# A graph kernel on one core: other due times for VectorE's order, a second buffer for the spread keys, one round fewer for the fourth block's list

## The chip, the cores and the metric

The kernel runs on one core of a Trainium2 chip. The metric is the device time of one execution in microseconds (us). The profile is one execution recorded on the chip; its times are counted from the first instruction of that execution. Engines are named as in the profile: PE is TensorE, PEld its weight loads, DVE is VectorE, ACT is ScalarE, POOL is GpSimd, SP is SyncE, which issues most plain DMAs.

## What is computed

Sixteen graphs of 1024 nodes with 64 channels go through four layers. Each layer adds to `x` a function of `relu(layernorm(x))` and of the graph's adjacency matrix. Cut to what matters:

```python
h = relu(layernorm(x)); x = x + tanh(concat(h, adj @ h) @ W1 + b1) @ W2 + b2      # layer 0
h = relu(layernorm(x)); A = adj + eye; x = x + (A @ h) / A.sum(2)                 # layer 1
h = relu(layernorm(x))                                                            # layer 2
# neighbours (adj > 0, with the node itself), thinned: of a node with m > 10 neighbours
# every ((m + 1) // 2)-th is removed, in both directions
# agg[n, c] = 0.25 q25 + 0.5 q50 + 0.25 q75 of h[neighbours of n, c]   (interpolated)
x = x + mask * (relu((h + agg) @ W1 + b1) @ W2 + b2)
h = relu(layernorm(x)); x = x + (adj @ h) / deg @ Wn + h @ Ws + b                 # layer 3
```

Layer 2 is the costly one. It needs the quantiles of each channel over a ragged set of neighbours.

## The kernel before

The nodes of a graph are put in the order of their number of neighbours and cut into 8 blocks of 128. Blocks share five groups (`GROUPS`), which hold 1, 1, 2, 2 and 2 blocks; `PLACES` says how many neighbours a block's nodes can have, 21 for the first down to 11 for the last. Per graph, six generator functions do the work:

- `adjacency` reads the matrix in 8 pieces, transposes it on TensorE into `adjt` (L947, copied by ScalarE in L948), counts neighbours (L954), works out the thinning (`gone`, L993 and L998), forms a key for each pair of nodes (L1018, L1022, L1025) and writes the keys to DRAM. Then it ranks the nodes: `key` and `neg` (L1032, L1034), two tiles `spread` (L1038) that TensorE turns into a matrix (L1040), eight passes `sink` on ScalarE that count (L1045), then `pos`, `low`, `both` (L1048 to L1062), a matmul (L1065) and `node` (L1071).
- `neighbour_lists` gathers each block's keys (`k`, POOL, L1086), takes the 8 largest with MAX8 (L1101) and then, in rounds of L1110 or L1112, L1115 and L1117, 8 more at a time. The list becomes `index`.
- `layers` does layers 0 and 1. Both hold a product with the adjacency matrix, `messages`: 32 matmuls L875 and a copy L876. The second one is issued after the `memset` L1197; behind it come L1202 and L1204 on TensorE, `den` on VectorE (L1217), and on ScalarE eight passes L1210 that sum degrees, each pair followed by a DMA that writes `adjt` to DRAM (`adjt_d`). A layer normalisation is `preln`: L846 to L848 on VectorE, the square L849 on ScalarE, L851 on VectorE, the root L852 on ScalarE, L854 and L855 on VectorE, L856 on ScalarE.
- `gathers` issues 124 gathers of neighbour rows (`raw`, POOL, L1274), one for each place of each block.
- `sorts` sorts `raw` by a network of minima and maxima on VectorE (L1307) and forms `agg` (L1324, L1326).
- `tail` brings `agg` back to node order (`res`, POOL, L1346), does the rest of layer 2 (`paired`: L883 on TensorE and L885 on ScalarE; L1355, L1356, then `per_node`: L899) and adds it to `x` on VectorE (`mid`, L1360); then layer 3, whose last product is read in L1395.

The engines run through their queues in the order in which instructions were issued, so the order of issue is the plan. It is made when the program is built. Each function is a generator that yields the time at which it wants to go on, worked out from a planned clock: `clk.dve`, `clk.pe`, `clk.act` and `clk.pool` are moved on by written costs, and `after(dve, pe, act, lat)` returns the moment when a chain over these engines should be done, plus `lat`. A loop at the end takes, in a fixed order of the six streams, the first one whose time has come; if none is due, the planned clock of VectorE jumps to the soonest. So the written costs decide what VectorE does between the issue of work for another engine and the instruction that reads its result. They are not waits: at run time an instruction waits for its data alone.

`gate` keeps POOL in step. VectorE writes a mark (L915) and POOL copies it (L917), so that POOL can't pass this place before VectorE has reached it. A gate is issued ahead of every fourth place of a group whose last mark lies over 4 us of planned time back.

Buffers come from pools. In the pool `lists` a tile has two buffers unless it says otherwise; `maskf`, `edge`, `spread`, `sink` and `low` share the tag `ab`, which has one. `adjt`, `nb` and `gone` have one each, and so has each group's `raw`.

Of the kernel before, what the change touches and what calls it, by code (L numbers as in the profile page):

```python
# [7 lines left out]
F32 = mybir.dt.float32  # L8
F16 = mybir.dt.float16
BF = mybir.dt.bfloat16  # L10
I32 = mybir.dt.int32
U16 = mybir.dt.uint16
U8 = mybir.dt.uint8
AF = mybir.ActivationFunctionType
ALU = mybir.AluOpType
AX = mybir.AxisListType

P = 128
C = 64
NB = 8  # L20
N = 1024
# [12 lines left out]
I16 = mybir.dt.int16  # L34
# [21 lines left out]
PLACES = [21, 19, 17, 16, 15, 13, 12, 11]  # L56
PACKS, NPACK = [(0, 0, 21, 2, 64), (1, 0, 23, 1, 32), (1, 32, 24, 4, 24), (2, 0, 28, 10, 12)], 3
KB = 4

# [670 lines left out]
def direct_path(ctx: ExitStack, tc: tile.TileContext, t: dict, out: bass.AP, flag):  # L730
# [3 lines left out]
    nc = tc.nc  # L734
    x_in, adj, nodemask = t["x"], t["adj"], t["nodemask"]
    B = x_in.shape[0]
# [64 lines left out]
    nc.gpsimd.dma_start(mask8, nodemask.rearrange("b (i p) -> (b i) p", p=P))  # L801
    maskf = lists.tile([B * NB, P], F32, tag="ab", name="maskf", bufs=1)
    nc.vector.tensor_copy(maskf, mask8)
# [10 lines left out]
    clk = Clock()  # L814
# [26 lines left out]
    def preln(u, x, ha):  # L841

        s = nodes.tile([P, 4, NB], F32, name="stat")
        xc = mid(u, [P, NB, C])
        sq = mid(u, [P, NB, C])
        nc.vector.tensor_reduce(s[:, 0], x, AX.X, ALU.add)  # L846
        ts(s[:, 1], s[:, 0], 1.0 / C, None, op0=ALU.mult)
        tt(xc, x, s[:, 1, :, None].to_broadcast([P, NB, C]), ALU.subtract)  # L848
        act(sq, xc, AF.Square)  # L849
        yield after(1.5, act=0.65)  # L850
        nc.vector.tensor_reduce(s[:, 2], sq, AX.X, ALU.add)  # L851
        act(s[:, 3], s[:, 2], AF.Sqrt, bias=eps, scale=1.0 / C)  # L852
        yield after(0.7, act=1.0)
        nc.vector.reciprocal(s[:, 2], s[:, 3])  # L854
        tt(xc, xc, s[:, 2, :, None].to_broadcast([P, NB, C]), ALU.mult)  # L855
        act(ha[:, :, :C], xc, AF.Relu)  # L856
        yield after(0.9, act=0.65)
# [20 lines left out]
    def paired(hs, dst):  # L878

        p = bank()  # L880
        for q in range(4):
            for e, h in enumerate(hs):
                nc.tensor.matmul(p[:, q * P:(q + 1) * P], h[:, 2 * q:2 * q + 2, :].rearrange("p u c -> p (u c)"), identf,  # L883
                                 start=e == 0, stop=e == len(hs) - 1)
        nc.scalar.copy(dst, p)  # L885
        clk.pe = max(clk.pe, clk.dve) + 1.5
        clk.act = max(clk.act, clk.pe) + 0.7
# [45 lines left out]
    def adjacency(b):  # L933
# [26 lines left out]
        sf = nodes.tile([P, 4, NB], F32, name="sf")  # L960
        yield clk.act + 0.3
        tt(mn[:, 2], mn[:, 0], mn[:, 1], ALU.add)
# [20 lines left out]
        for i in range(NB):  # L983
            following = flipped(i + 1) if i + 1 < NB else None

            p = bank2()
            for j in range(NB):
                o, e = j * P, (j // 4 + 1) * 512
                nc.tensor.matmul(p[:, o:e], nbt[:, j, :], stair[:, :e - o], start=j % 4 == 0, stop=j % 4 == 3)  # L989

            for q in range(2):
                s = slice(q * 512, (q + 1) * 512)
                act(gone[:, i, s], p[:, s], AF.Abs, bias=sf[:, 2 + q, i:i + 1], scale=2.0)  # L993
            nbt = following
            ready = after(0, pe=3.7, act=2.4)
            if waiting:
                yield waiting[1]
                ts(gone[:, waiting[0], :], gone[:, waiting[0], :], sf[:, 1, waiting[0]:waiting[0] + 1], -1.0,  # L998
                   op0=ALU.is_equal, op1=ALU.mult)
                clk.dve += 0.5  # L1000
            waiting = (i, ready)
# [27 lines left out]
        act(mv, ms, AF.Copy, bias=512.0, scale=0.5)  # L1029
        yield clk.act + 0.3  # L1030
        key = nodes.tile([P, NB], F32, name="key")
# [4 lines left out]
        for q in range(2):  # L1036
            spread = lists.tile([P, 4, P], F32, tag="ab", name="spread", bufs=1)
            tt(spread, identf[:, None, :].to_broadcast([P, 4, P]),  # L1038
               key[:, 4 * q:4 * q + 4, None].to_broadcast([P, 4, P]), ALU.mult)
            nc.tensor.matmul(p[:, q * 512:(q + 1) * 512], onesf, spread.rearrange("p j m -> p (j m)"),  # L1040
                             start=True, stop=True)
        over = nodes.tile([P, NB], F32, name="over")
        for i in range(NB):
            sink = lists.tile([P, N], F16, tag="ab", name="sink", bufs=1)
            act(sink, p, AF.Sign, bias=neg[:, i:i + 1], accum_out=over[:, i:i + 1])  # L1045
        yield after(1.6, pe=1.3, act=10.5)
        pos = nodes.tile([P, NB], I32, name="pos", bufs=5)
# [6 lines left out]
        nc.vector.tensor_copy(ph, pi)  # L1054
        low = lists.tile([P, NB, P], F16, tag="ab", name="low", bufs=1)
        tt(low, pidx[:, None, :].to_broadcast([P, NB, P]), ph[:, 0, :, None].to_broadcast([P, NB, P]), ALU.is_equal)
# [11 lines left out]
        nc.scalar.copy(m, p[:, NB:2 * NB])  # L1068
        yield after(2.3, pe=1.2, act=0.2) - 0.2
        node = nodes.tile([P, NB], I32, name="node", bufs=3)  # L1070
# [6 lines left out]
    def neighbour_lists(b):  # L1077
# [3 lines left out]
        ks = []  # L1081
# [9 lines left out]
        for i in range(KB):  # L1091
            load_keys(i)
        total = sum(n * -(-cap // 8) * 8 for _, n, cap, *_ in GROUPS)
        found = lists.tile([P, total], F32, name="found", bufs=1)
        m = g["m"]
        o = 0
        for b0, n, cap, *_ in GROUPS:
            for i in range(b0, b0 + n):
                src, at = ks[i]
                yield at  # L1100
                nc.vector.max(out=found[:, o:o + 8], in_=src)  # L1101
                clk.dve += 1.15
                yield clk.dve
                less, before = src.bitcast(I16), None
                for r in range(1, -(-cap // 8)):


                    least = found[:, o + 7:o + 8]
                    if r == 1:
                        ts(less, src, least, None, op0=ALU.subtract)  # L1110
                    else:
                        ts(less, less, before, least, op0=ALU.add, op1=ALU.subtract)  # L1112
                    before = least
                    most = nodes.tile([P, 8], U16, name="most")
                    nc.vector.max(out=most, in_=less.bitcast(U16))  # L1115
                    o += 8
                    ts(found[:, o:o + 8], most.bitcast(I16), 0.0, least, op0=ALU.min, op1=ALU.add)  # L1117
                    clk.dve += 1.8
                    yield clk.dve
                o += 8  # L1120
                load_keys(i + KB)
        index = lists.tile([P, total], I32, name="index")
# [51 lines left out]
    def layers(b):  # L1174
# [17 lines left out]
        nc.scalar.copy(x, p)  # L1192
        yield after(0, pe=1.3, act=2.1) + 2.8
        ha = nodes.tile([P, NB, C + 1], F32, name="ha")
# [18 lines left out]
        done.add(("adjt", b))  # L1213
        yield after(0, pe=10.5, act=1.1) + 2.5
        clk.act += 10
# [21 lines left out]
    def gathers(b):  # L1237
        g = state[b]
        yield max(g["rows_at"], clk.pool)
        for k, (b0, n, cap, *_) in enumerate(GROUPS):  # L1240
            while not (b == 0 or ("sort", b - 1, k) in done):
                yield None
            raw = raws.tile([P, cap, n * C], F32, name=f"raw{k}")
            o = sum(c * -(-r // 8) * 8 for _, c, r, *_ in GROUPS[:k])
            clk.pool = max(clk.pool, clk.dve)
# [6 lines left out]
            if k == 0:  # L1252
                packed = nodes.tile([P, NPACK * C], F32, name="packed", bufs=1)
                for l, size in enumerate(sizes):
                    nc.gpsimd.indirect_dma_start(packed[:size, l * C:(l + 1) * C], None, h_ds[b % 3],
                                                 bass.IndirectOffsetOnAxis(ap=g["pack"][:size, l:l + 1], axis=0))
                    clk.pool += 1.27
                rows_d = dram.tile([NPACK, P, C], F32, name="rows_d")
            for s in range(cap):
# [9 lines left out]
                for i in range(n):  # L1269
                    if s >= PLACES[b0 + i]:  # L1270
                        continue
                    clk.pool += 1.27
                    at = o + i * -(-cap // 8) * 8 + s
                    nc.gpsimd.indirect_dma_start(raw[:, s, i * C:(i + 1) * C], None, h_ds[b % 3],  # L1274
                                                 bass.IndirectOffsetOnAxis(ap=g["index"][:, at:at + 1], axis=0))
# [64 lines left out]
    def tail(b):  # L1340
# [16 lines left out]
        y = per_node(bank(), h1, w22, 8, b22)  # L1357
        yield after(0, pe=2.2, act=1.5) + 3.2
        o = mid(1, [P, NB, C])
# [17 lines left out]
        nc.scalar.copy(x, per_node(bank(), ht, w3s, 4, b3, x))  # L1377
        yield after(0, pe=3, act=0.6, lat=0.5)

# [12 lines left out]
        zn = per_node(bank(), mt, w3n, 4)  # L1392
        yield after(0, pe=2.6)
        o = mid(1, [P, NB, C])
# [16 lines left out]
    programs = [_program(*group[2:]) for group in GROUPS]  # L1411
    edge = lists.tile([1, 2, C], F32, tag="ab", name="edge", bufs=1)
    nc.vector.memset(edge[:, 0], 0.0)
# [165 lines left out]
```

## Time and profile before

| | us |
|---|---|
| median of 7 runs | 3699.97 |
| lowest, highest | 3697.49, 3700.79 |
| the profiled execution | 3697.76 |
| its span, first to last instruction | 3695.8 |
| VectorE busy | 3067.9 |
| POOL busy | 2600.5 |
| TensorE busy | 1977.2 |
| ScalarE busy | 1420.6 |

A line of the profile names the kernel's line, the engine, the operation and the tiles, written tile first; behind the bar it has the busy time, the mean of one instruction in ns, and the idle time of the engine just before it with what ended it. In an answer on waits, "DVE a L1 <- PE b L2: 10.0, 4, 3.0" says that VectorE stood idle ahead of L1 for 10.0 us in all, 4 times and 3.0 us at most, until TensorE's L2 was done. Issuing a DMA is not counted as busy, and a gather's own record is the time that POOL spends on it. The largest groups of VectorE:

```profile
L1307 DVE TENSOR_TENSOR other<-raw 128x512 f32<-128x512 f32 (+11 forms) x816 | 536.3, 689 | 47.8 <-DMA raw<-h_d,index 34.6 <-DVE agg L1326 1.6 <-DVE mark L915 0.7
L1115 DVE MAX8 most<-k 128x8 uint16<-128x1024 uint16 x224 | 275.1, 1228 | 7.7
L1112 DVE TENSOR_SCALAR k<-k,found 128x1024 int16<-128x1024 int16 x96 | 55.8, 581 | 2.3
L1117 DVE TENSOR_SCALAR found<-most,found 128x8 f32<-128x8 int16 x224 | 56.3, 251 | 8.0
```

### The profile page before, as it was taken

The numbers are of one execution on the slowest core, as the hardware profiler recorded it, in microseconds if no ns is written. First come the engines' busy times: TensorE is split into PE (matmuls) and PEld (weight loads), VectorE is DVE, ScalarE is ACT, GpSimd is POOL, SyncE is SP. The second block draws the span as 40 slices with busy tenths as digits, with TensorE's granted clock in tenths as the row PEclk, the third lists the DMA queues.
The fourth block names the chain that finished last, engine by engine and source line by source line (L and its number), as shares of the span: only waits on it lengthen the run. The fifth ranks groups of instructions, "written<-read, shape, count | busy, mean of one in ns | idle before, by whom it ended". The sixth has DMA issues, their size and how long they took to land.

```text
span 3695.8 us, 32061 instructions
## 1 busy us (share of the span) xinstructions
PE 1977.2 (53%) x8483; PEld 959.5 (26%) x8483; DVE 3067.9 (83%) x7173; ACT 1420.6 (38%) x2658; POOL 2600.5 (70%) x2608
## 2 busy tenths in 40 slices
PE   6563756456555456465564575455656564634033
PEld 3322332222313123132221323122232322312011
DVE  2658889798789989879796999969878798998982
ACT  6534444343434434253343435334443443521000
POOL 1177777678677877768677677857868677777871
PEclk9776767677667677676667766676766667766555
DMA  2314252342525343252432425334252433324121
GB/s 94 131 46 134 53 173 64 107 111 69 154 52 158 82 118 115 42 169 56 134 98 79 125 63 147 81 107 112 61 162 56 145 88 95 105 52 129 42 55 58
DMA packets 237344, 362.40 MB, mean 98 GB/s; under 512 B 126848, under 2 KB 128496, under 8 KB 237152
## 3 DMA queue, kind: packets, MB, share of 16 engines
q1 hardware_dynamic: 156912, 255.00, 20.2%
q0 software_dynamic: 80096, 104.70, 14.4%
q8 instruction: 69, 1.13, 0.1%
q14 instruction: 123, 1.01, 0.1%
q10 hardware_dynamic: 144, 0.56, 0.0%
HBM read 245.26 MB, written 114.81 MB: 97 GB/s over the span
## 4 chain that ended last, share of the span: by engine, by line
DVE 59%; PE 13%; POOL 9%; issue 7%; DMA 7%; ACT 5%; DVEq 0%; SPq 0%; POOLq 0%; ACTq 0%
DVE other L1307 16%; DVE raw L1307 15%; PE pt L875 8%; POOL raw L1274 8%; DVE most L1115 6%; DVE found L1101 3%; DVE agg L1326 3%; DMA adjt_d<-adjt 2%; ACT adjt L1210 2%; DMA raw<-h_d,index 2%; DVE k L1110 1%; DVE nb L940 1%; DVE found L1117 1%; DVE k L1112 1%; PE pt L899 1%
## 5 line engine op out<-in xcount | busy, mean ns | idle before, releaser
L1274 POOL DMA_INDIRECT raw<-h_d,index x1984 | 2171.0, 1094 | 572.1 <-issue 528.3
L1307 DVE TENSOR_TENSOR other<-raw 128x512 f32<-128x512 f32 (+11 forms) x816 | 536.3, 689 | 47.8 <-DMA raw<-h_d,index 34.6
L875 PE MATMUL pt<-adjt,ha 128*65 128x512 f32 (+1 forms) x1024 | 491.9, 642 | 157.0 <-DVE ha L1197 148.1
L1307 DVE TENSOR_TENSOR raw<-other 128x512 f32<-128x512 f32 (+10 forms) x464 | 356.4, 792 | 5.3
L947 PE MATMUL pt<-ef,a 128*128 128x128 f32 x1024 | 202.8, 363 | 251.9 <-ACT adjt L948 206.4
L989 PE MATMUL pt<-eh,nbt 128*128 128x512 f16 (+3 forms) x1024 | 193.3, 341 | 172.3 <-ACT nbt L978 171.9
L1115 DVE MAX8 most<-k 128x8 uint16<-128x1024 uint16 x224 | 275.1, 1228 | 7.7
L875 PEld LDWEIGHTS pt<-adjt,ha 128*65 128x65 f32 (+1 forms) x1024 | 149.3, 149 | 479.5 <-issue 407.0
L1022 ACT ACTIVATE nb<-pt 128x1024 f16<-128x1024 f32 x128 | 130.5, 1019 | 330.1 <-PE pt L1018 287.5
L1086 POOL DMA_INDIRECT k<-keys_d,node x128 | 131.9, 1031 | 175.8 <-DVE node L1071 113.0
L1018 PE MATMUL pt<-eh,gone 128*128 128x128 f16 x1024 | 135.1, 263 | 195.3 <-DVE gone L998 123.1
L947 PEld LDWEIGHTS pt<-ef,a 128*128 128x128 f32 x1024 | 164.7, 191 | 285.6 <-ACT adjt L948 239.2
L1307 DVE TENSOR_TENSOR raw<-other,raw 128x640 f32<-128x640 f32 (+3 forms) x448 | 217.2, 495 | 4.9
L876 ACT COPY big<-pt 64x1024 f32<-64x1024 f32 (+1 forms) x32 | 32.2, 1007 | 482.4 <-PE pt L875 482.4
L1307 DVE TENSOR_TENSOR raw<-raw,other 128x128 f32<-128x128 f32 (+7 forms) x496 | 212.4, 437 | 5.8
L917 POOL COPY gate<-mark 1x1 f32<-1x1 f32 x293 | 96.2, 328 | 169.5 <-DVE mark L915 167.2
L954 ACT ACTIVATE nb<-nb 128x512 f16<-128x512 f16 x256 | 159.8, 631 | 131.9 <-DVE nb L942 68.9
L948 ACT COPY adjt<-pt 128x512 f32<-128x512 f32 x256 | 137.8, 584 | 180.7 <-DMA adjt_d<-adjt 99.5
L1307 DVE TENSOR_TENSOR other<-other,raw 128x128 f32<-128x128 f32 (+4 forms) x448 | 201.6, 460 | 3.9
L993 ACT ACTIVATE gone<-pt,sf 128x512 f16<-128x512 f32 x256 | 163.4, 696 | 72.4 <-DVE sf L968 56.6
L1346 POOL DMA_INDIRECT res<-agg_d,pos x128 | 135.3, 1057 | 62.2 <-issue 34.8
L1045 ACT ACTIVATE sink<-pt,neg 128x1024 f16<-128x1024 f32 x128 | 142.4, 1113 | 88.4 <-PE pt L1040 84.7
(182 smaller groups left out, 4277.7 us busy)
## 6 DMA issues: line engine op xcount, KB each, us to landing
a<-in_adj_dram SPq DMA_DIRECT2D x64, 1024.0 KB
adjt_d<-adjt SPq DMA_DIRECT2D x64, 1024.0 KB
at<-adjt_d SPq DMA_DIRECT2D x128, 512.0 KB
keys_d<-nb SPq DMA_DIRECT2D x64, 512.0 KB
raw<-h_d,index POOLq DMA_INDIRECT x1984
x<-in_x_dram SPq DMA_DIRECT2D x16, 256.0 KB
h_d<-h SPq DMA_DIRECT2D x16, 256.0 KB
agg_d<-agg SPq DMA_DIRECT2D x16, 256.0 KB
```

Of the source, the lines that this page charges most:

```text
L875: nc.tensor.matmul(p[p0:p0 + n, s], h[:, j, :n], adjt[:, j, s], start=j == 0, stop=j == NB - 1)
L947: nc.tensor.transpose(p[:, u * P:(u + 1) * P], a[:, j * P:(j + 1) * P], identf)
L948: nc.scalar.copy(adjt[:, 4 * q:4 * q + 4, i * P:(i + 1) * P], p.rearrange("p (u m) -> p u m", m=P))
L954: act(nb[:, i, s], nb[:, i, s], AF.Copy, accum_out=mn[:, q, i:i + 1])
L989: nc.tensor.matmul(p[:, o:e], nbt[:, j, :], stair[:, :e - o], start=j % 4 == 0, stop=j % 4 == 3)
L993: act(gone[:, i, s], p[:, s], AF.Abs, bias=sf[:, 2 + q, i:i + 1], scale=2.0)
L1018: nc.tensor.matmul(p[:, d], gone[:, j, i * P:(i + 1) * P], big_i, start=False, stop=j == 4 * q + 3 and i // 4 != q)
L1045: act(sink, p, AF.Sign, bias=neg[:, i:i + 1], accum_out=over[:, i:i + 1])
L1115: nc.vector.max(out=most, in_=less.bitcast(U16))
L1274: nc.gpsimd.indirect_dma_start(raw[:, s, i * C:(i + 1) * C], None, h_ds[b % 3], bass.IndirectOffsetOnAxis(ap=g["index"][:, at:at + 1], axi ...
L1307: tt(view(two[to], *((i, vi) if greater else (j, vj)), w), view(two[s], i, vi, w), view(two[u], j, vj, w), ALU.max if greater else ALU.min)
L1346: nc.gpsimd.indirect_dma_start(res[:, i, :], None, g["agg_d"], bass.IndirectOffsetOnAxis(ap=g["pos"][:, i:i + 1], axis=0))
```

## The change

Three things are changed.

First, the planned clock. Most results that come from TensorE or ScalarE are planned to be there later, by 1 to 7 us, and POOL's DMAs are planned at 1.39 us in place of 1.27. Instructions stay the same; their order on each engine's queue does not.

Second, the tag `ab` has the pool's two buffers in place of one.

Third, the rounds of a block's list come from a new table `LISTS`. Before, they followed from the group's capacity, which made 24 places for the fourth block (index 3); now it has 16, which is what `PLACES` lets it use. The other blocks keep their rounds; the loop over groups and blocks becomes one over blocks.

```diff
+LISTS = [40, 24, 24, 16, 16, 16, 16, 16]
...
-    maskf = lists.tile([B * NB, P], F32, tag="ab", name="maskf", bufs=1)
+    maskf = lists.tile([B * NB, P], F32, tag="ab", name="maskf")
...
-        yield after(1.5, act=0.65)
+        yield after(1.5, act=0.65, lat=1.2)
...
-        yield after(0.7, act=1.0)
+        yield after(0.7, act=1.0, lat=1.5)
...
-        clk.pe = max(clk.pe, clk.dve) + 1.5
+        clk.pe = max(clk.pe, clk.dve) + 2.0 * len(hs)
...
-        yield clk.act + 0.3
+        yield clk.act + 4.0
...
-            ready = after(0, pe=3.7, act=2.4)
+            ready = after(0, pe=3.7, act=2.4, lat=3.0)
...
-        yield clk.act + 0.3
+        yield clk.act + 2.0
...
-            spread = lists.tile([P, 4, P], F32, tag="ab", name="spread", bufs=1)
+            spread = lists.tile([P, 4, P], F32, tag="ab", name="spread")
...
-            sink = lists.tile([P, N], F16, tag="ab", name="sink", bufs=1)
+            sink = lists.tile([P, N], F16, tag="ab", name="sink")
...
-        yield after(1.6, pe=1.3, act=10.5)
+        yield after(1.6, pe=1.3, act=10.5, lat=2.0)
...
-        low = lists.tile([P, NB, P], F16, tag="ab", name="low", bufs=1)
+        low = lists.tile([P, NB, P], F16, tag="ab", name="low")
...
-        yield after(2.3, pe=1.2, act=0.2) - 0.2
+        yield after(2.3, pe=1.2, act=0.2) + 1.5
...
-        total = sum(n * -(-cap // 8) * 8 for _, n, cap, *_ in GROUPS)
+        total = sum(LISTS)
...
-                for r in range(1, -(-cap // 8)):
+            for r in range(1, LISTS[i] // 8):
...
-        yield after(0, pe=1.3, act=2.1) + 2.8
+        yield after(0, pe=3.4, act=2.1) + 7.0
...
-        yield after(0, pe=10.5, act=1.1) + 2.5
+        yield after(0, pe=14.0, act=1.1) + 6.0
...
-                    clk.pool += 1.27
+                    clk.pool += 1.39
...
-                    clk.pool += 1.27
-                    at = o + i * -(-cap // 8) * 8 + s
+                    clk.pool += 1.39
+                    at = sum(LISTS[:b0 + i]) + s
...
-        yield after(0, pe=2.2, act=1.5) + 3.2
+        yield after(0, pe=6.5, act=2.1) + 6.0
...
-        yield after(0, pe=3, act=0.6, lat=0.5)
+        yield after(0, pe=3.5, act=0.6, lat=3.0)
...
-        yield after(0, pe=2.6)
+        yield after(0, pe=2.6, lat=5.0)
```

More of the change, by code (lines that the diff above doesn't have):

```diff
@@ L1096, in neighbour_lists @@
         o = 0
[L1097 to L1102, printed above, removed]
-                yield clk.dve
-                less, before = src.bitcast(I16), None
-                for r in range(1, -(-cap // 8)):
[L1108 to L1121, printed above, removed]
+        for i in range(NB):
+            src, at = ks[i]
+            yield at
+            nc.vector.max(out=found[:, o:o + 8], in_=src)
+            clk.dve += 1.15
+            yield clk.dve
+            less, before = src.bitcast(I16), None
+            for r in range(1, LISTS[i] // 8):
+                least = found[:, o + 7:o + 8]
+                if r == 1:
+                    ts(less, src, least, None, op0=ALU.subtract)
+                else:
+                    ts(less, less, before, least, op0=ALU.add, op1=ALU.subtract)
+                before = least
+                most = nodes.tile([P, 8], U16, name="most")
+                nc.vector.max(out=most, in_=less.bitcast(U16))
+                o += 8
+                ts(found[:, o:o + 8], most.bitcast(I16), 0.0, least, op0=ALU.min, op1=ALU.add)
+                clk.dve += 1.8
+                yield clk.dve
+            o += 8
+            load_keys(i + KB)
         index = lists.tile([P, total], I32, name="index")
@@ L1243, in gathers @@
             raw = raws.tile([P, cap, n * C], F32, name=f"raw{k}")
-            o = sum(c * -(-r // 8) * 8 for _, c, r, *_ in GROUPS[:k])
             clk.pool = max(clk.pool, clk.dve)
@@ L1411, in direct_path @@
     programs = [_program(*group[2:]) for group in GROUPS]
-    edge = lists.tile([1, 2, C], F32, tag="ab", name="edge", bufs=1)
+    edge = lists.tile([1, 2, C], F32, tag="ab", name="edge")
     nc.vector.memset(edge[:, 0], 0.0)
```

## The prediction

> **What bounds the kernel now.** I read the page's first part, the waits of VectorE, the waits of POOL, and then one graph on the timeline, because a list of waits names the last releaser and not what held that releaser up.
>
> ```profile
> span 3695.8 us, 32061 instructions
> PE 1977.2 (53%) x8483; PEld 959.5 (26%) x8483; DVE 3067.9 (83%) x7173; ACT 1420.6 (38%) x2658; POOL 2600.5 (70%) x2608
> ...
> DVE 59%; PE 13%; POOL 9%; issue 7%; DMA 7%; ACT 5%; DVEq 0%; SPq 0%; POOLq 0%; ACTq 0%
> ...
> DVE mid L1360 <- PE pt L899: 173.5, 11, 24.2
> DVE spread L1038 <- PE pt L1040: 106.9, 16, 15.7
> DVE den L1217 <- PE pt L1204: 47.1, 13, 4.9
> DVE other L1307 <- DMA raw<-h_d,index: 34.6, 9, 26.1
> ...
> POOL raw L1274 <- issue: 528.3, 1844, 0.6
> POOL gate L917 <- DVE mark L915: 167.2, 36, 21.0
> ```
>
> VectorE (DVE) is busy for 3067.9 us and idle for 627.9. Its waits add up to 524 us in the answer on waits, so some 104 us are gaps too short to be listed. Three waits on TensorE make 327.5 of the 524: `mid` in `tail`, `spread` in `adjacency`, `den` in `layers`. Data of the gathers hardly ever hold VectorE: 34.6 us, of which 26.1 are the first one.
>
> POOL looks freer than it is. A gather takes 1094 ns and is followed by 0.286 us of issue (528.3/1844), 1.38 us in all. From the first gather (192.7 us) to the last (about 3611) POOL stood still for about 177 us, 167.2 of them at gates that VectorE had not reached. Without any of these, the same starts and the same 86 us behind the last gather give 3695.8 - 177 = 3519 us. That is the floor that POOL sets, 5% below the present span.
>
> The 18 us waits of `mid` show their cause in graph 8; first VectorE, then ScalarE (ACT) in the same stretch:
>
> ```profile
> 1787.51 0.21 DVE L1217 RECIPROCAL den<-pt 128x8 f32<-128x8 f32 x1 [4.04 <-PE pt L1204]
> ...
> 1813.99 0.69 DVE L1360 TENSOR_TENSOR mid<-pt,mask 128x512 f32<-128x512 f32 x1 [18.45 <-PE pt L899]
> ```
> ```profile
> 1783.97 1.01 ACT L876 COPY big<-pt 65x1024 f32<-65x1024 f32 x1 [15.90 <-PE pt L875]
> 1784.88 1.05 ACT L1210 ACTIVATE adjt<-adjt 128x1024 f32<-128x1024 f32 x1
> ...
> 1792.17 1.04 ACT L1210 ACTIVATE adjt<-adjt 128x1024 f32<-128x1024 f32 x1
> ...
> 1803.44 1.07 ACT L948 COPY adjt<-pt 128x512 f32<-128x512 f32 x2 [10.14 <-DMA adjt_d<-adjt]
> ...
> 1805.64 0.58 ACT L885 COPY mid<-pt 128x512 f32<-128x512 f32 x1
> 1808.38 1.26 ACT L1356 ACTIVATE big<-pt,L_gnn_b 128x512 f32<-128x512 f32 x2 [2.16 <-PE pt L1355]
> ```
>
> The wait is named after TensorE, but ScalarE is what was late. It stands 15.9 us at L876 for the second messages, makes the degree sums (L1210, 8.2 us), then stands 10.1 us at L948 until `adjt` is written out, and only then gets to L885, which `mid` needs. VectorE has only about 8 us of work between `den` and `mid`.
>
> **What the Trainium skill says.** "PSUM — Partial Sum Buffer", Engine vs sequencer instructions: the queues of ScalarE, VectorE and GpSimd are strict FIFO and matmuls complete in program order. The trace agrees: L885 stood ready behind L948 for 10.1 us. "Perfetto Trace Analysis", DMA Instruction — SWDGE (GPSIMD): the recorded time of such a DMA is the generating of descriptors, not the moving of data. It agrees too: a POOL row of 1094 ns, and data that land 2.3 to 3.5 us into the chain of waits. So POOL's rate is a cost of its own that VectorE's order cannot lower.
>
> **The change, part by part.** T is the moment of VectorE's `memset` L1197 in a graph, with which the second messages start. From graph 8 (T = 1768.38): L876 starts at T+15.6, `den` is ready at T+19.1, L1210 ends at T+24.9. Two matmul pairs L1040 take 2.2 us and eight sinks L1045, 1.24 us apart, 9.3 to 9.9. "Cover" below is VectorE work between two places in the built order, priced with the mean durations of these rows.
>
> *Block 3 of the list.* `LISTS` gives it 16 places in place of 24: 16 rounds go, each L1112 + L1115 + L1117 = 0.58 + 1.23 + 0.25 us. 16 x 2.06 = 33 us off VectorE, the fuller engine. The gathers stay 1984, since `PLACES` sets them: nothing off POOL.
>
> *Two buffers of tag `ab`.* The second spread no longer waits for the first one's matmul. That ends 91.7 us of the 106.9 (15.2 are graph 0's). It makes no TensorE work earlier; what is late next is `pos`, which needs both matmuls and the sinks.
>
> *New latencies.* They cost no instruction; they move them. In the old order `mid` stood 6 to 9 us of cover behind `den` in nine graphs. In the new one it stands, in ten of thirteen, between 11 us ahead of T and 18 us behind, so that L885 and L1356 are issued ahead of L876 and of the block at L948; in the other three it is 34 to 38 us behind T, with the sinks where the block was. So the 149.3 us of `mid` before the last graph go, all but 2. `den` now has 16 to 19 us of cover in place of 15: 47.1 us shrink to about 9.
>
> But `spread` moves too. In the old order it stood 21 to 51 us of cover ahead of T from graph 3 on; in eight graphs of the new order it stands 0 to 4 us behind T. Its matmuls then queue behind the second messages, its sinks behind L876 and L1210, and the `Square` L849 of `tail` behind L1210 also. New waits, as in graphs 3, 4, 5 and 11: L851 comes at T+16 to 18 but can't run before T+25.7, so 8 to 9 us; then `pos` comes 4.5 to 6.4 us later and needs T+34.5, so another 3 to 5. Going through graphs 1 to 15 in the built order in this way I get 3, 7, 12, 14, 12, 15, 18, 2, 0.5, 15, 11, 5, 8, 12 and 3 us: 137. In graphs 7 and 10, where the spread is ahead of the messages, the node matmuls L1065 are behind them, and `node` and L854 wait instead. So 149.3 + 91.7 + 47.1 = 288 us of waits become 137: 151 less. Bounds: 137 is a sum of differences against a moment that I took from one graph; 90 if the small gaps between instructions cover 3 us more in each, 190 if the messages start 4 us later.
>
> *Start.* `mn` now follows L846, which waits for `x`: 36.8 becomes 41.4 us. The spread of graph 0 follows its `den`. First gather about 5 us later.
>
> *POOL.* The cost 1.39 in place of 1.27 places each sort just where the plan's gather lands. Counting 1.385 us per POOL DMA from a gate to the end of a group, against cover from that gate to the sort: in the old order graphs 1 to 14 mostly have 10 to 130 us to spare, in the new one groups 0 and 2 have -4 to +5. Over a whole graph POOL then needs about 10 us more than the cover; the 137/15 = 9 us of waits on ScalarE lie in the same stretch and nearly hide it. I charge 18 us for all middle graphs (0 to 120). In the last graph nothing hides it: from its first gates POOL needs 60 to 65 us more than VectorE has work. Charge 60, against 5.8 now: +55, and 6 for graph 0's fourth group, whose sort moves ahead.
>
> **Sum.** 3695.8 - 33 - 151 + 5 + 6 + 55 + 18 = 3596 us. The other count must agree: POOL's floor 3519 + 4 (start) + about 20 for `pack` and other waits that remain + 13 graphs of 208 - 204 us lost at gates = 3595. Around the span lie 2.0 us (3697.76 of that execution), and the median of the runs is 2.2 us above it: 3600 us.
>
> **Rivals.**
> 1. VectorE's waits vanish nearly (the cover is larger than I price it). Then POOL alone bounds: 3519 + 5 + 20 = 3544, and 3548 as a median. For: POOL is a queue that needs only data. Against: L1210 stands ahead of the sinks in the built order.
> 2. The two engines hold each other up: VectorE's wait stops POOL at a gate, POOL's lateness stops VectorE at the next group. With 5 us more in each of 13 graphs: 3596 + 65 = 3661, median 3665. For: spare time near zero in groups 0 and 2. Against: the stall and the gap lie in one stretch.
> 3. Slower. The same mechanism at full size: sorts wait for `raw` in every graph because POOL no longer runs ahead. It decides from (3703 - 3596)/13 = 8 us per middle graph on top of mine; at the full 10 us of POOL's excess it gives 3596 + 130 = 3726, median 3730. For: the lead of 10 to 130 us is given away. Against: it needs the 9 us of ScalarE waits to hide nothing.
> 4. The order does nothing of weight: if the new waits reach 260 us, with list and end as above, 3596 + 123 = 3719, beside rival 3.
>
> **How the numbers follow.** Forecast (3560 to 3635): 0.53. Rival 1: 0.19. Rival 2: 0.14. Rivals 3 and 4 on the slow side 0.11, and 0.03 within 0.2% (7 us, about what a measurement here can tell from no change). Faster: 0.53 + 0.19 + 0.14 = 0.86. Of the range, the low end is rival 1's floor, 3540; the high end takes in rival 2, 3675; some 0.15 lies outside, mostly above.
>
> **What would show it.** Right: `mid L1360` and `spread L1038` nearly gone from VectorE's waits (below 30 us each), new entries `stat L851 <- ACT mid L849`, `pos L1048 <- ACT sink L1045`, `stat L854` or `node L1071` of 100 to 170 us together; L1115 down from 224 to 208; `other L1307 <- DMA raw` up from 34.6 to about 120, much of it after 3300 us; the gate wait of POOL below 100. Wrong: `raw` waits of over 200 us (rivals 2 and 3), or hardly any new wait on ScalarE (rival 1).

## The result and the profile after

| | before | after |
|---|---|---|
| median, us | 3699.35 (33 runs) | 3687.10 (13 runs) |
| lowest, highest, us | 3690.06, 3705.45 | 3682.77, 3690.06 |
| ratio after/before | | 0.9967, 95% interval 0.9960 to 0.9974 |
| span of the profiled execution, us | 3695.8 | 3682.6 |

The changed kernel is 12 us faster (0.3%, and the interval leaves out 1), where 100 were forecast. Its lines of code have numbers two higher than in the kernel before up to about L1100, then one higher, and from L1255 on the same. The top of the page, then the engines of the chain that ended last:

```profile
span 3682.6 us, 32083 instructions
PE 1999.7 (54%) x8483; PEld 974.8 (26%) x8483; DVE 3036.2 (82%) x7137; ACT 1404.5 (38%) x2658; POOL 2585.8 (70%) x2620
...
DVE 60%; POOL 16%; issue 9%; DMA 8%; PE 4%; ACT 3%; SPq 0%; DVEq 0%; POOLq 0%; ACTq 0%
```

VectorE's work fell by 31.7 us, as forecast (33). Its idle time did not fall but rose, from 627.9 to 646.4 us. In the chain TensorE went from 13% to 4% and POOL from 9% to 16%: the end no longer hangs on matmul results, but on gathers. VectorE's waits (total, times, longest):

```profile
DVE other L1307 <- DMA raw<-h_d,index: 136.8, 20, 22.5
DVE stat L853 <- ACT mid L851: 62.3, 12, 11.0
DVE pos L1050 <- ACT sink L1047: 42.4, 9, 10.6
DVE gone L1000 <- ACT gone L995: 34.1, 9, 15.7
DVE found L1102 <- DMA k<-keys_d,node: 30.7, 10, 5.0
DVE den L1218 <- PE pt L1205: 28.2, 3, 23.0
DVE stat L856 <- ACT stat L854: 26.6, 6, 11.9
...
DVE mid L1360 <- PE pt L901: 24.4, 2, 24.1
DVE node L1073 <- ACT m L1070: 23.9, 3, 16.1
```

The three waits on TensorE that made 327.5 us are down to 52.6, and most of what is left of `mid` is one wait in the last graph. Four waits on ScalarE (`stat` twice, `pos`, `node`) came instead: 155 us, before 29. `raw` went from 34.6 to 136.8. That leaves VectorE where it was. POOL's waits:

```profile
POOL packed L1255 <- DMA pack<-pack_d: 99.6, 17, 23.1
POOL gate L919 <- DVE mark L917: 61.3, 27, 5.6
POOL packed L1255 <- issue: 52.0, 24, 13.2
```

Gates cost POOL 106 us less than before. But it now waits for 152 us ahead of `packed`, the first gathers of a graph, whose row numbers (`pack`) are made from the list (`index`) of that graph by small DMAs; before, the two lines held 56. In both kernels some 23 to 26 us of this are graph 0's. For the 52.0 us marked `issue` the profile names no releaser, so the order of the records has to tell. The timeline between the gathers of graphs 3 and 4 shows one such wait (start, duration, instruction, idle before it in brackets): the list is written at 1046 us, 3 us after POOL's last gather of graph 3, its DMAs follow, and POOL goes on at 1054. POOL, then VectorE, then SyncE:

```profile
1042.14 0.95 POOL L1274 DMA_INDIRECT raw<-h_d,index  x1 [0.31 <-issue]
1054.11 1.05 POOL L1255 DMA_INDIRECT packed<-h_d,pack  x1 [11.02 <-issue]
1056.44 0.95 POOL L1255 DMA_INDIRECT packed<-h_d,pack  x1 [1.28 <-DMA pack<-pack_d]
```
```profile
1045.80 0.25 DVE L1128 TENSOR_TENSOR index<-none,found 128x84 int32<-128x84 f32 x1
```
```profile
1046.08 2.15 SPq L1132 DMA_DIRECT2D pack_d<-index  x4
1049.77 3.13 SPq L1134 DMA_DIRECT2D pack<-pack_d  x3
```

VectorE's timeline a little earlier, in the same graph, suggests why the list is late:

```profile
962.15 0.17 DVE L1050 TENSOR_SCALAR pos<-over 128x8 int32<-128x8 f32 x1 [4.11 <-ACT sink L1047]
...
970.91 0.16 DVE L1073 CAST node<-pt 128x8 int32<-128x8 f32 x1
970.98 0.68 DVE L942 TENSOR_SCALAR nb<-a 128x1024 f16<-128x1024 f32 x1
```

The first adjacency row of graph 5 (L942) comes right behind `node` of graph 4. In every graph it is so: `adjacency` runs as a closed loop, rows, `mn`, `gone`, `key`, `pos`, `node`, rows. One turn of it takes 208 us on average (the records of L1073), and POOL, without its stops, needs about 201 for a graph. In the kernel before, the rows mostly came with the second messages of `layers`, on average 21 us behind `node` for the nodes of graphs 3 to 13, and the list was ready 39 us (mean over graphs 2 to 14, from the records that write `index` and those of L1274) before POOL had ended the graph ahead. After, this time is 9 us, and in 8 of 15 graphs there is none. Below I call it the lead of the list.

### The profile page after: what moved, and what is told of

Same layout as the page of the kernel before. It is cut to its first block, busy times and chain, and to the rows that moved or that the text cites. A ratio compares the mean times of both kernels' runs of the same rounds, so it can differ in the third digit from the quotient of the medians.

```text
span 3682.6 us, 32083 instructions
## 1 busy us (share of the span) xinstructions
PE 1999.7 (54%) x8483; PEld 974.8 (26%) x8483; DVE 3036.2 (82%) x7137; ACT 1404.5 (38%) x2658; POOL 2585.8 (70%) x2620
## 4 chain that ended last, share of the span: by engine, by line
DVE 60%; POOL 16%; issue 9%; DMA 8%; PE 4%; ACT 3%; SPq 0%; DVEq 0%; POOLq 0%; ACTq 0%
DVE raw L1307 16%; DVE other L1307 16%; POOL raw L1274 14%; DVE most L1116 7%; DMA raw<-h_d,index 4%; DVE found L1102 4%; DVE agg L1326 2%; PE pt L877 2%; DMA k<-keys_d,node 2%; DVE k L1111 2%; DVE nb L942 1%; DVE found L1118 1%; DVE k L1113 1%; DVE gone L1000 1%; ACT adjt L1211 1%
## 5 line engine op out<-in xcount | busy, mean ns | idle before, releaser
L1274 POOL DMA_INDIRECT raw<-h_d,index x1984 | 2143.4, 1080 | 565.0 <-issue 522.2
L1307 DVE TENSOR_TENSOR other<-raw 128x512 f32<-128x512 f32 (+11 forms) x816 | 536.4, 689 | 211.2 <-DMA raw<-h_d,index 136.8
L877 PE MATMUL pt<-adjt,ha 128*65 128x512 f32 (+1 forms) x1024 | 485.7, 636 | 119.0 <-DVE ha L1198 66.5
L991 PE MATMUL pt<-eh,nbt 128*128 128x512 f16 (+3 forms) x1024 | 222.0, 377 | 365.3 <-ACT nbt L980 365.1
L1116 DVE MAX8 most<-k 128x8 uint16<-128x1024 uint16 x208 | 255.4, 1228 | 7.2
L991 PEld LDWEIGHTS <-nbt 128*128 128x128 f16 x1024 | 108.0, 119 | 463.6 <-ACT nbt L980 379.1
L949 PEld LDWEIGHTS pt<-ef,a 128*128 128x128 f32 x1024 | 152.0, 180 | 283.0 <-ACT adjt L950 170.0
L1383 PE MATMUL tm<-at,ha 128*64 128x512 f32 x512 | 173.6, 777 | 46.8 <-DMA at<-adjt_d 46.5
L1020 PE MATMUL pt<-eh,gone 128*128 128x128 f16 x1024 | 120.6, 243 | 137.4 <-DVE gone L1000 75.0
L885 PE MATMUL pt<-ef,res 128*128 128x128 f32 x128 | 38.6, 396 | 278.7 <-DMA res<-agg_d,pos 278.7
L1102 DVE MAX8 found<-k 128x8 f32<-128x1024 f16 x128 | 156.3, 1221 | 30.7 <-DMA k<-keys_d,node 30.7
```

What stands on the lines that cost most here:

```text
L877: nc.tensor.matmul(p[p0:p0 + n, s], h[:, j, :n], adjt[:, j, s], start=j == 0, stop=j == NB - 1)
L949: nc.tensor.transpose(p[:, u * P:(u + 1) * P], a[:, j * P:(j + 1) * P], identf)
L1307: tt(view(two[to], *((i, vi) if greater else (j, vj)), w), view(two[s], i, vi, w), view(two[u], j, vj, w), ALU.max if greater else ALU.min)
L1383: nc.tensor.matmul(p[q * C:(q + 1) * C, :], ha[:, j, :], even(ats[j], q), start=j == 0, stop=j == NB - 1)
```

## The experiments

Lists and buffers, each alone, on the kernel before:

```diff
-        total = sum(n * -(-cap // 8) * 8 for _, n, cap, *_ in GROUPS)
+        total = sum(LISTS)
...
-                for r in range(1, -(-cap // 8)):
+                for r in range(1, LISTS[i] // 8):
```

> The kernel before with the shorter list of the fourth block alone. If VectorE's work bounds the kernel before (as I predicted), all of the 33 us that the 16 rounds cost comes off: about 3666 us. If a loop of waits through several engines sets the time of a graph, VectorE idles a little longer elsewhere and less than a third of it comes off: 3688 to 3699 us.

3635.11 us, ratio 0.9826 (0.9811 to 0.9842): 62 us less, nearly twice the work that it takes away. Neither reading had foreseen that. POOL's gates fell from 167.2 to 79.8 us.

```diff
-            spread = lists.tile([P, 4, P], F32, tag="ab", name="spread", bufs=1)
+            spread = lists.tile([P, 4, P], F32, tag="ab", name="spread")
```

(and so for the other tiles of the tag.)

> The kernel before with two buffers of the tag ab alone, same order on VectorE. The 106.9 us of waits of the second spread go. If VectorE's waits are lost time, some 50 to 90 us come off (a part comes back at pos): 3610 to 3650 us. If they were slack in a loop that something else closes, under 15 us: 3685 to 3699 us.

3648.55 us, ratio 0.9878 (0.9863 to 0.9893): 48 us less, with gates of 109.6 us. So either of these two parts alone does four to five times what the whole change does. The new due times must give something back. First suspect, the price, which is the planned cost of a gather of `raw` or `packed` (POOL's other DMAs keep theirs), taken back in the changed kernel:

```diff
-                    clk.pool += 1.39
+                    clk.pool += 1.27
```

> The changed kernel with POOL's planned cost back at 1.27 us in place of 1.39, all else as changed. Theory A (the higher cost places each sort just where its data land, and the two engines hold each other up): the lead of the gathers comes back, waits for raw on VectorE fall from about 140 to under 60 us, time 3600 to 3640 us. Theory B (POOL stands at the packed gathers because a graph's index is finished only as POOL ends the graph before, and 8 us of small DMAs lie between): the index is no earlier by this, time within 15 us of the changed kernel's 3687.

3772.78 us, ratio 1.0206 (1.0192 to 1.0219): 86 us slower than the changed kernel. Theories A and B both failed: in the changed kernel the higher price helps. POOL's waits of this run:

```profile
POOL packed L1255 <- DMA pack<-pack_d: 157.4, 20, 22.5
POOL packed L1255 <- issue: 133.6, 24, 23.5
...
POOL gate L919 <- DVE mark L917: 5.5, 2, 2.8
```

No gate stops POOL any more; it waits for lists instead, which are now 13 us late on average. Second suspect, the trip of the packed row, put off in the changed kernel from the start of the first group to its eleventh place:

```diff
-            if k == 0:
+                if k == 0 and s == 10:
                     packed = nodes.tile([P, NPACK * C], F32, name="packed", bufs=1)
...
-                if k == 0 and s == 9:
+                if k == 0 and s == 15:
...
-                if k == 0 and s == 17:
+                if k == 0 and s == 20:
```

> The changed kernel with the three packed gathers of a graph issued behind 10 of the first group's 21 gathers instead of ahead of them, and the DMAs that pass their rows on issued 3 to 6 places later. Theory B: POOL's waits at packed (some 150 us with those put down to issue, 11 us in most graphs) fall below 40, since the 8 us of small DMAs then lie beside gathers; with POOL bound, 60 to 100 us come off: 3590 to 3625 us. Theory A, or a theory that the new waits on ScalarE ate the gain: the waits at packed go but the time stays within 15 us of 3687.

3677.89 us, ratio 0.9953 (0.9940 to 0.9967), some 9 us below the changed kernel, with intervals that overlap. The waits went, and the gates took them back:

```profile
POOL gate L919 <- DVE mark L917: 162.9, 50, 18.7
```

That is 102 us more at the gates than the changed kernel has. Here, letting POOL start a graph sooner only sends it into the next gates sooner. The wait for `pack` is therefore not by itself what sets the time: what is taken away there comes back at the gates. The next four runs take the due times apart: e5 is the change without any of them, e6 is e5 with 1.39, and e7 and e8 are the changed kernel with a part of the due times as before.

```diff
-        yield clk.act + 4.0
+        yield clk.act + 0.3
...
-            ready = after(0, pe=3.7, act=2.4, lat=3.0)
+            ready = after(0, pe=3.7, act=2.4)
...
-        yield clk.act + 2.0
+        yield clk.act + 0.3
...
-        yield after(1.6, pe=1.3, act=10.5, lat=2.0)
+        yield after(1.6, pe=1.3, act=10.5)
...
-        yield after(2.3, pe=1.2, act=0.2) + 1.5
+        yield after(2.3, pe=1.2, act=0.2) - 0.2
```

This is e7; e8 does the same with `paired` and the due times in `layers` and `tail`. The two due times of `preln`, the layer normalisation, stay new in both.

> The kernel before with the shorter lists and the second buffer of the spread keys, every due time as it was: the change without its new due times. Taken alone the lists took 62 us off and the buffer 48. Theory C (the later due times of the adjacency stream give back what the two other parts won): 3575 to 3610 us, if the two gains add, and in any case at least 50 below the changed kernel. Theory D (the later due times of the layers and the tail give it back): the same here. Theory E (the two parts win the same time twice, because the gathers of POOL bound it from there on): about 3635.

> As e5, with POOL's gathers planned at 1.39 us in place of 1.27. If the planned pitch of the gathers is what pays for itself (raw waits short, the sorts of the ring never early), 10 to 40 us below e5. If a plan with slow gathers puts work late that could go early, 10 to 50 above e5. Theories C and D both leave it within 20 of e5.

> The changed kernel with the five due times of the adjacency stream (mn, gone, key, pos, node) as they were before. Theory C: the rows of a graph, its list and its packed row come earlier against POOL, the waits for raw fall from 137 us below 70, and the time is 3590 to 3630. Theory D: within 20 us of the changed kernel's 3687.

> The changed kernel with the due times of the layers, the paired passes and the tail (tx, zt, den, y, zn, mid) as before, those of the adjacency stream new. Theory D: 3590 to 3630 us. Theory C: within 20 us of 3687, with the waits for mid's matmul back at over 80 us.

e5: 3597.30 us, ratio 0.9729 (0.9716 to 0.9742). The two gains add nearly fully, and the due times of the change give 90 us back. e6: 3746.07, ratio 1.0127 (1.0111 to 1.0142): the price of 1.39 alone costs 149 us here, three times the most that was expected, where e3 had it gain 86. e7: 3694.47, ratio 0.9990 (0.9981 to 0.9998), and e8: 3721.63, ratio 1.0062 (1.0048 to 1.0076): neither part alone is to blame. Theory C failed in its number, though the lists came much earlier in e7 (104 us ahead), and theory D failed too. POOL's gates in e5, then in e6:

```profile
POOL gate L919 <- DVE mark L917: 55.3, 13, 18.6
```
```profile
POOL gate L919 <- DVE mark L917: 246.7, 49, 23.4
```

VectorE's waits for `raw` are the same in both (62.3 and 66.5 us). With 1.39 in the plan VectorE doesn't wait more for gathers; POOL waits more for VectorE. Four more runs complete the picture, two with 1.27 and a part of the due times new, and two with a lower price:

> Lists, buffers and the new due times of layers and tail, with the adjacency's due times and POOL's planned 1.27 us as before. Theory F: the planned 1.39 us alone gives back some 150 us (3746 against 3597), because with gathers that slow the plan sees VectorE idle, runs the other streams out to their limits, and leaves no work to put into the waits on the chip; the adjacency's new due times give back about as much by another way, its serial loop. Under F this kernel has neither and is at 3560 to 3620, the waits for mid and den together below 90 us. Theory G (the new due times of layers and tail are tuned to 1.39 and cost at 1.27): 3650 or more.

> Lists, buffers and the new due times of the adjacency stream, with those of layers and tail and POOL's planned 1.27 us as before. Theory F with the serial loop: 3650 to 3780, rows of graph b+1 start at node of graph b and not at the second messages, POOL waits for packed on pack in most graphs. If the loop is harmless without the new due times of the layers: 3590 to 3630.

> e5 with POOL's gathers planned at 1.15 us, less than they take. Theory F says that a plan without idle time on VectorE keeps POOL fed: the gates' waits (55 us in e5) shrink, the waits for raw grow from 62; the time is within 25 us of e5's 3597 and not, as at 1.39, 150 above. If what counts is that the planned pitch is right, it is worse than e5 by 30 or more.

> e9 with POOL's gathers planned at 1.15 us. Same reading as e11 against e5: within 25 us of e9 under F; 30 or more above e9 if the planned pitch has to be the true one.

e9: 3571.93 us, ratio 0.9671 (0.9653 to 0.9689), faster than the changed kernel by 115. e10: 3696.82, ratio 1.0002 (0.9994 to 1.0010): the new due times of the adjacency and of `preln` cost 100 us against e5, and the rows start at `node` there, as expected. e11 and e12 at 1.15: 3760.96, ratio 1.0178 (1.0164 to 1.0192), and 3797.39, ratio 1.0268 (1.0251 to 1.0285). Theory F, that a plan without idle time is good as such, fell with these two: the low price costs 164 us against e5 and 225 against e9, more than the high one (149 and 123), and mostly by the other kind of wait. POOL in e11:

```profile
POOL packed L1255 <- DMA pack<-pack_d: 222.2, 20, 23.5
...
POOL gate L919 <- DVE mark L917: 71.2, 10, 12.1
```

So 1.15 and 1.39 both lose against 1.27, although a gather takes 1.38 us on the chip. Theory H offers a reason: the plan prices VectorE's own work too low as well. e5 spends about 3147 us on this work and the short gaps in it, outside the listed waits, and the written costs add up to 2912; 3147/2912 is 1.08, and 1.38/1.08 is 1.28. By the plan's own measure of time, 1.27 is then nearly right and 1.39 is 9% too slow. e17 tests it: e7's kernel, with 1.39, and every cost of VectorE times 1.08. e18 is e9 with 1.29, to show how much a difference may owe to the chance of an order. (e13 and e14, named in what was expected, are the same two kernels at another time; they come further down.)

```diff
-        clk.dve += dve
+        clk.dve += 1.08 * (dve)
...
-                clk.dve += 0.085 + size / 960
+                clk.dve += 1.08 * (0.085 + size / 960)
```

> The kernel of e13 on a chip where the kernel before takes its usual time. Theory H (what counts is the ratio of POOL's price to VectorE's in the plan): 3560 to 3620, the gates' waits below 70 us. If 1.39 as such is what hurts: within 25 us of e7's 3694, gates at about 160.

> The kernel of e14, 1.29 in place of e9's 1.27. Theory H: 3550 to 3610. A distance of more than 40 us from e9's 3572 would say that the chance of an order is as large as the effects that are read here.

e17: 3598.11 us, ratio 0.9728 (0.9715 to 0.9741), 96 below e7, at the same 1.39. e18: 3570.13, ratio 0.9651 (0.9638 to 0.9664), 2 us from e9. So, with these due times, 1.39 does no harm as such; out of scale with VectorE's prices it does. The scale is not all, since e17 and e18 have it alike (1.39/1.08 is 1.287) and differ by 28 us. e17's gates are a little above the 70 us expected of them:

```profile
POOL gate L919 <- DVE mark L917: 76.2, 37, 7.8
```

e18 beats both kernels, and the changed one by 117 us. At the place where the changed kernel had POOL idle for 11.02 us (here between the gathers of graphs 4 and 5) it goes straight on, and the next graph's first row (L942) comes together with the second messages (L1198), 45 us after `node` of graph 4 (at 881 us), so that the row no longer waits for `node`:

```profile
1217.85 0.94 POOL L1274 DMA_INDIRECT raw<-h_d,index  x1 [0.30 <-issue]
1219.10 1.80 POOL L1255 DMA_INDIRECT packed<-h_d,pack  x1 [0.30 <-issue]
```
```profile
925.78 0.74 DVE L942 TENSOR_SCALAR nb<-a 128x1024 f16<-128x1024 f32 x1
925.81 0.07 DVE L1198 MEMSET ha<- 128x8 f32 x1
```

The runs above with both buffers and short lists side by side. "New" and "old" are due times, where those of `preln` are old in e5, e6 and e11 alone; the waits are POOL's in us, the lead is that of the list, as above:

| run | adjacency | layers, tail | price | us | gates | `packed` | lead |
|---|---|---|---|---|---|---|---|
| e5 | old | old | 1.27 | 3597 | 55 | 48 | 57 |
| e9 | old | new | 1.27 | 3572 | 27 | 92 | 17 |
| e18 | old | new | 1.29 | 3570 | 55 | 43 | 48 |
| e17 | old | new | 1.39, VectorE x 1.08 | 3598 | 76 | 38 | 52 |
| e4 | new | new | 1.39, `packed` later | 3678 | 163 | 11 | 20 |
| changed kernel | new | new | 1.39 | 3687 | 61 | 152 | 9 |
| e7 | old | new | 1.39 | 3694 | 160 | 45 | 104 |
| e10 | new | old | 1.27 | 3697 | 2 | 231 | -5 |
| e8 | new | old | 1.39 | 3722 | 104 | 61 | 87 |
| e6 | old | old | 1.39 | 3746 | 247 | 42 | 114 |
| e11 | old | old | 1.15 | 3761 | 71 | 230 | 1 |
| e3 | new | new | 1.27 | 3773 | 6 | 291 | -13 |
| e12 | old | new | 1.15 | 3797 | 3 | 348 | -12 |

The four fast ones have POOL waits of 98 to 119 us in the two columns together, all others 165 to 351. POOL issues the same DMAs in all of them, so this sum is the account of the time and not yet its cause. The four also have a lead of 17 to 57 us. Of the others, a lead far above 60 goes with gates and one near or below zero with late lists. But a lead in between is not enough: e4 has 20 us and still 163 us of gates, and the kernel before, with its longer list and single buffer, 39 us and 167 of gates. What the lead does show is the sign of two effects. The price lengthens it in all four pairs that differ in nothing else (e5 and e6, e9 and e7, e10 and e8, e3 and the changed kernel), the adjacency's later due times shorten it (e9 and e3: from 17 to -13; e7 and the changed kernel: from 104 to 9). This fits that these due times cost 201 us by themselves (e3 against e9) and the higher price 123 (e7 against e9), but both together only 115 (the changed kernel): they partly cancel.

Four runs made somewhat earlier for the price question, e13 to e16, can't be read against the others: at that time the kernel before itself took 4032.89 us in place of 3696 to 3700. e13 is e17's kernel, e14 is e18's, and two are others:

> e7 (3694 us: lists, buffers, new due times of layers and tail, old ones of the adjacency, POOL planned at 1.39) with every cost of VectorE in the plan times 1.08. 1.08 is e5's VectorE time outside its listed waits, about 3147 us, over the 2912 us that the plan charges for it. Theory H (what counts is the ratio of POOL's price to VectorE's): 3560 to 3620, near e9's 3572, gates below 70 us in place of 160. If 1.39 as such is what hurts: within 25 us of e7.

> e9 with 1.29 in place of 1.27. Theory H: 1.39/1.08 is 1.287, so this is the balanced price; 3550 to 3610. The difference to e9 shows how much of a few tens of us is the chance of an order.

> e9 with 1.33. Theory H: between e9 (3572) and e7 (3694), 3600 to 3660, and the gates' waits between 27 and 160 us. If it is as fast as e9, the loss comes between 1.33 and 1.39 and is no matter of a ratio.

> e9 with the three gathers of the packed row at s == 10 of the first group, and what follows from them later too, as in e4. e9's POOL waits 71 us there on the index of the packed row, 25 of them in graph 0. If POOL is the bound: 20 to 45 us below e9's 3572, which would be the fastest kernel. If the wait comes back at the gates or at the first gather of raw, as in e4: within 15 us of e9.

e13 gave 3977.70 us, ratio 0.9868 (0.9821 to 0.9915), e14 3958.40, ratio 0.9801 (0.9764 to 0.9837), e15 3919.49, ratio 0.9714 (0.9671 to 0.9758), e16 4020.39, ratio 0.9978 (0.9953 to 1.0003). Of these, 1.33 is the fastest, with an interval apart from that of 1.29. It was not run in the usual time, so where between 1.27 and 1.39 the best price lies is not shown, nor what the later packed row does otherwise.

## Why the prediction was wrong

- *Lists:* 33 us of work forecast, 31.7 measured. Shown; the time gained by it alone was larger (62 us in e1), with 87 us fewer at POOL's gates. Why the order came out so was not taken apart.
- *Waits on TensorE:* `spread` gone, `mid` down to the last graph's, `den` 28.2 us in place of about 9, of which 23.0 are one wait in graph 0. Right but for that one.
- *New waits on ScalarE:* 137 us forecast, 126 more than before measured, on the four tiles named. Right in mechanism and size: on these two counts VectorE waits 149 us less, forecast 151.
- *Raw:* about 114 us forecast (34.6 + 6 + 55 + 18), 136.8 measured. The size is not far off, the reason was: "The cost 1.39 in place of 1.27 places each sort just where the plan's gather lands" made the higher price the source of waits for `raw`. e6 has them at 66.5 with 1.39, beside 62.3 in e5; the changed kernel with 1.27 has not fewer but 247.0 (e3). In e6 the price works by POOL's gates. Only 35.7 us of `raw` fall after 3300 us, where the forecast put 60.
- *The step that failed* is the term "about 20 for `pack` and other waits that remain" in the check by POOL's floor. It takes the lists to be ready in time. The two waits ahead of `packed` hold 152 us, some 130 of them after graph 0, where the kernel before had about 30. The gates were well sized: 13 graphs of 4 us forecast, 61.3 us measured (the forecast does not say how it came to 208 and 204). Counted by the gaps in POOL's own records beyond a normal issue, it stood still for about 182 us between its first and its last gather of `raw` (117 ahead of `packed`, 59 at gates, 6 at `k`), where the forecast has 72. The rest of that stretch took 3213 us, before 3234, mainly because a gather took 1080 ns in place of 1094. Whether the order made the gathers shorter is not shown: two executions of one order differ by 7 ns (e14 and e18). 110 us more of stops less 21 make 89, close to the 86 us by which the span missed 3596. I had read the waits around T off the order and had not asked when the next graph's list is ready, so I did not see that its lead of 39 us was being spent.
- *The parts.* In the forecast's own terms (an estimate), list and buffers give 33 + 92 = 125 us, and due times and price together cost about 25 (137 + 84 of new waits less 149 and 47). Measured, list and buffers give 101 (e5) and due times and price cost 90. The sign of both was in the forecast, the size of the second was not.
- *The sum on VectorE* hid it. There 288 us of waits were to become 137, with 84 added elsewhere. Measured, all listed waits together went from 524 to 540. Besides 23 us more of `raw` than forecast, the sorts' other waits (`packed` 11.5, `rows_d` 4.7, issue 19.4, `mid` L887 25.8) and `gone` (+17) had been put at nothing. That the two counts agreed within 1 us was no proof: both had waits missing, and each took the other engine's waits as given. e4 takes away POOL's waits for `pack` and gains some 9 us by it.
- *Rivals:* the result lies above rival 2 (3665), which had the right kind, two engines that hold each other up, but put it into sorts and gates and not into late lists. Rival 3's place, `raw` in every graph, did not show: 52 us of its 136.8 fall between 1000 and 3300 us (33.4 up to 2000 and 18.4 after).
- *The signs.* Nearly all the signs that were named for being right came: `spread` gone, `mid` at 24.4, 155 us on ScalarE, L1116 down to 208, `raw` at 136.8, the gates at 61.3. None of them watched POOL's wait for a list, so they could all come true and the time still be wrong.
- *Two small readings:* the last gather starts 85 us before the end, not 86, and L1210 lasts 8.4 us in graph 8, not 8.2. Neither changes a sum.

What stays open: why one order has a lead of 17 us and another of 57 at the same price (e9, e5) with a better time for the shorter one, and why e4's lead of 20 us does not help it. That late lists and gates are how the due times and the price cost their 90 us is read from the waits; that due times and price do cost them is shown by taking them out.

## What to carry to other kernels

Prices in a planned clock should be in one scale. Here the true duration of a gather beside VectorE prices that are 8% low made the order worse by 123 to 149 us with the adjacency's old due times (e9 and e7, e5 and e6), and scaling VectorE's prices took 96 of it back (e17). It is no rule for every order: with the adjacency's new due times and the other new ones the same higher price gained 86 us (e3 and the changed kernel). Where two engines feed each other through a list or a gate, look at the lead of each hand-over and at the waits on both sides together, before and after: in e4 a wait taken away on one side came back on the other. And when a change has several parts, run each alone and in pairs. Here list and buffers were worth 101 us together. Later due times helped in one set (e9 against e5: 25 us) and harmed in another (e3 against e9: 201 us), and the adjacency's, so harmful at 1.27, gained 7 us at 1.39 (the changed kernel against e7).

## What the runs showed of the hardware

At the time of the longer runs (e13 to e16) the instructions of VectorE and POOL were no slower. For one kernel (price 1.29) a gather took 1079 ns then (e14) and 1086 in e18, and MAX8 1228 ns in both. TensorE was slower: 2112.0 us busy against 2010.9, with a granted clock of 0.667 against 0.699. That is 101 us on an engine that is busy little more than half of the time, and the span is 398 us longer, so most of the difference is waiting. POOL's gates alone went from 55.1 to 391.4 us. The chain of that run puts a share to something outside the core's own engines:

```profile
DVE 41%; issue 14%; another core or an unknown queue 13%; PE 11%; ACT 8%; POOL 7%; DMA 5%; SPq 0%; DVEq 0%; ACTq 0%; POOLq 0%
```

In e18 the same kernel's chain has no such entry. What it was, the traces don't say.
